# A graph network on one core: ScalarE's and VectorE's pieces laid anew beside TensorE's products

## The chip, the cores and the metric

The kernel runs on one core of one Trainium2 chip, in float32 throughout. The metric is the device time of an execution in microseconds; the time before is the median of three runs. The profile is of one further execution.

## The reference, cut to what matters

Sixteen graphs of 1024 nodes with 512 features each (x), one weighted adjacency matrix adj (1024 x 1024) for all, and two layers with a residual each:

```
# layer 0
h = relu(layernorm(x))
x = x + (adj @ h) @ W0 + bias
# layer 1
u  = relu(layernorm(x))
s1 = (u @ W) @ a1 ; s2 = (u @ W) @ a2
e  = leaky_relu(s1[:, None] + s2[None, :], 0.2) * adj
z  = softmax(e) @ (u @ W) + beta * (u @ W)
x  = x + elu(z)
```

## The kernel before

**Strassen products.** Each big product is done in Winograd's form: seven half-size products p1 to p7 of blocks and of sums of blocks. A left side has the blocks A11, A12, A22, S1 to S4, a right side B11, B21, B22, T1 to T4. In layer 0 the left is h, transposed by the product itself, and the right is the transposed adjacency (adjT); the result y (blocks C11, C12, C21, C22 and their S sums) is the left of a second product with W0 (`Weighted`), whose seven products are added to the residual x one at a time (`to_residual`). Layer 1 has the same two steps with the softmax in place of adjT (tiles pT) and W1 in place of W0.

**Batches in order.** First layer 0 runs for batches 0 to 15, then layer 1 for batches 0 to 15. Each batch of layer 0 has two phases:

- `layer0_a` (batch 0, plain products, 14 half products, "slots" 0 to 13) or `layer0_a2` (batches 1 to 15). In the second, p1, p5, p3 and p4 are split once more into seven small products r1 to r7 (*inner products*), and each is interleaved with a plain one, step by step: p1 with p2, p5 with p6, p3 with p7, p4 with the first product of W0. That gives 4 x 7 = 28 slots, 0 to 27. The loop is at lines 274 to 302. After r1, r5 and r7 ScalarE copies a small result out of PSUM (y_p1t, y_p5t, ... ; r5's copy goes into a buffer named in_p); r6, r7 and r3 end in sums on VectorE. r6 writes into r1's PSUM tile and so waits for r1's copy, and r7 waits for r6's sum. p6 and p7 accumulate in the banks Y that p1 has begun, and so wait until p1's (then p6's) partial result is copied to C11 (C12).
- `layer0_b`: what remains of the seven products with W0, in 14 slots of eight 256-wide matmuls. After each, VectorE adds PSUM to the residual tile xr. Batch 0 takes the products in the order of PRODUCTS (p1, p2, p6, p5, ...), all others in that of A12_LATE (p1, p5, p6, p2, p7, p3, p4).

**What sets the order beside the products.** Every engine takes its instructions in program order (`InOrder`). What ScalarE, VectorE, GpSimd and SP (which issues the DMAs) do beside TensorE is put by hand into *slots*: a plan maps a slot to steps, and `beside(plan)` emits those of slot k after the k-th piece of TensorE's work, slot -1 ahead of the phase. Of one slot, the sums that belong to the product come first, then the plan's. An instruction that waits holds up all behind it on its engine, and a DMA that waits holds up SP. The steps:

- `h_stats` (b, k, c), `h_relu`: layernorm statistics of x chunk k of the next batch (five ScalarE instructions, then small ones on GpSimd), and its normalization with relu on ScalarE. `h_sums`: the sums S1, S2, S4 of h, four VectorE additions for each half. `inner_left`: the sums of one left block for its inner product, four VectorE additions (tiles in_p). `load_x` loads a chunk of x into one of two buffers; `load_res` loads residual rows (xr) into one of four.
- Of `LayerOut` (the result of the batch before): `stats` and `relu` (ScalarE), `logits` (two VectorE products with sums against the vectors v), `sums` (VectorE) and `store` (SP); `keep` stores xr.
- `Softmax` of batch 0 is prepared early: batches 5 to 12 each do one row block g in layer0_b (load of the mask e{g}, M{g}: four ScalarE and four VectorE instructions, K{g}: store). Batch 13 takes the maxima (N, n). Batch 15 reloads the blocks (R{g}, DMA er<-ed) and exponentiates them (E{g}: four ScalarE exponentials, two VectorE transposes). D, d, S, s, T1a to T3b are the rest of the softmax and the sums of its blocks.
- In batch 0 also: `adj_sum` (T1 to T4 of adjT, two VectorE additions each), `w_sums`, `inner_right` (sums of a right block for its inner product, tiles ext), and `logit_weights` (eight VectorE products of W with a1 and a2, then a store vd<-v) with `logit_weights_back` (load of the resulting vectors into v_bc).

`in_fourteen` (line 1067) lays plans made for 28 slots on batch 0's 14 by halving the slot. At lines 1200 and 1201 the plan of slots 0 and 1 of layer0_b is taken over into slots 23 and 26 of layer0_a2.

**Buffers.** Pool b8 has ten slots of one h, adjT or pT block (or of W), b4 twelve smaller ones for y blocks, h sums, small results, masks and e rows; PSUM has eight banks. A tile that finds no free slot waits until one is given back.

## Time and profile before

| what | value |
|---|---|
| time, median of 3 | 2345.65 us (2345.25 to 2348.89) |
| profiled execution | 2345.13 us, span 2343.3 us |
| granted TensorE clock, mean | 0.995 |
| TensorE busy | 2294.7 us (98%) |
| VectorE / ScalarE / GpSimd busy | 1782.8 / 1496.8 / 582.9 us |
| layer 0, batch 0 | 0 to 98.5 us |
| layer 0, batches 1 to 15 | 98.5 to 1170 us |
| layer 1 | 1170 to 2343.3 us |
| DMA | 383.15 MB, mean 164 GB/s |

A line of a timeline has the start and the duration in microseconds, the engine, line, operation, output and inputs by their names in the program with buffer numbers left out, the shapes, how many instructions are merged, and in brackets the idle time ahead of it and what ended it. Line 111 is that of the helper through which every instruction is emitted, so lines are told apart by the tiles' names. In the table of waits, the columns are total, number and longest wait. Matmuls are pipelined and their ends modelled, so the start of one to the start of the next says more than their durations.

### The profile page before, as it was taken

The page shows a single profiled execution, that of the slowest core. Times are in us where ns is not written, and L with a number is a line of the kernel's source. Part 1 is how long each engine was busy: PE and PEld are TensorE (multiplying, and loading weights), DVE is VectorE, ACT ScalarE, POOL GpSimd, SP SyncE. Part 2 cuts the span into 40 slices and gives each one's busy share as a digit, 9 for nine tenths or more (in the row PEclk, how much of TensorE's full clock was granted, in tenths as well). Part 3 has the DMA queues.
Part 4 walks back from the last instruction along what each step waited for, and adds up shares of the span by engine and source line. Part 5 has one row for each costly group of instructions (what it writes and reads, how often), then busy time and mean ns, then how long its engine had stood idle before and what let it go on. Part 6 is the DMA issues. An engine that isn't in the chain of part 4 may idle for free.

```text
span 2343.3 us, 28480 instructions
## 1 busy us (share of the span) xinstructions
PE 2294.7 (98%) x7984; PEld 1511.0 (64%) x7984; DVE 1782.8 (76%) x3932; ACT 1496.8 (64%) x4025; POOL 582.9 (25%) x680
## 2 busy tenths in 40 slices
PE   9899999999999999999899999999999999999998
PEld 5677777777667777677655666556665566655665
DVE  4887777787777787877877787777877778777774
ACT  4565767665767666666357676666766677667743
POOL 1333223333223333232102221122211222102220
PEclk9999999999999999999999999999999999999999
DMA  6254544454543554433754556555565545555541
GB/s 229 64 189 153 171 151 131 153 189 145 171 150 124 168 189 145 163 120 123 245 184 155 166 178 206 173 178 166 189 211 173 186 159 167 179 182 166 175 128 44
DMA packets 207247, 383.15 MB, mean 164 GB/s; under 512 B 80240, under 2 KB 88432, under 8 KB 207088
## 3 DMA queue, kind: packets, MB, share of 16 engines
q1 hardware_dynamic: 206768, 380.81, 49.8%
q8 instruction: 63, 1.03, 0.2%
q14 instruction: 96, 0.79, 0.1%
q10 hardware_dynamic: 320, 0.52, 0.1%
HBM read 251.92 MB, written 133.50 MB: 164 GB/s over the span
## 4 chain that ended last, share of the span: by engine, by line
PE 60%; ACT 14%; DVE 13%; DMA 7%; issue 4%; SPq 2%; POOL 0%; ACTq 0%; DVEq 0%; POOLq 0%
PE z_Y L111 12%; PE y_Y L111 9%; PE pq_Y L111 6%; PE z_X L111 6%; PE po_Y L111 6%; ACT uS L111 5%; PE z_W L111 4%; PE pq_X L111 3%; PE y_X L111 3%; DVE e L111 2%; PE po_X L111 2%; DMA md<-mx 2%; ACT e L111 2%; PE po_W L111 2%; DVE hS L111 2%
## 5 line engine op out<-in xcount | busy, mean ns | idle before, releaser
L111 POOL TENSOR_TENSOR x<-x,r 128x512 f32<-128x512 f32 x120 | 226.0, 1894 | 874.7 <-DVE x L111 432.1
L111 ACT ACTIVATE e<-e,nm 128x256 f32<-128x256 f32 x480 | 237.4, 498 | 162.3 <-DVE nm L111 162.3
L111 DVE CUSTOM_DVE_ANT_0 e<-e,mask 128x256 f32<-128x256 f32 x512 | 233.2, 508 | 66.2 <-DMA mask<-maskd 34.8
L111 POOL TENSOR_TENSOR xr<-xr,bias_bc 128x512 f32<-128x512 f32 x128 | 168.2, 1336 | 269.0 <-DMA xr<-in_x_dram 182.8
L111 PE MATMUL z_Y<-pT,ul_U 128*128 128x512 f32 x512 | 224.9, 592 | 0.0
L111 ACT ACTIVATE e<-s2b,s1b 128x256 f32<-128x256 f32 x512 | 215.1, 506 | 9.0 <-DMA s2b<-s2d 9.0
L111 DVE STREAM_TRANSPOSE pT<-e 128x512 f32<-128x512 f32 x240 | 155.6, 686 | 67.4 <-ACT e L111 67.4
L111 PE MATMUL po_Y<-w_c,y_C 128*128 128x256 f32 x768 | 191.5, 384 | 3.8 <-DVE xr L111 3.8
L111 PE MATMUL pq_Y<-w_c,z_C 128*128 128x256 f32 x768 | 175.4, 380 | 0.6
L111 PEld LDWEIGHTS z_Y<-pT,ul_U 128*128 128x128 f32 x512 | 97.3, 190 | 115.6 <-issue 111.7
L111 DVE CUSTOM_DVE_ANT_0 uS<-xr,v_bc 128x512 f32<-128x512 f32 x240 | 165.7, 691 | 6.2
L111 ACT ACTIVATE r<-z,rs 128x256 f32<-128x256 f32 x192 | 95.7, 499 | 110.9 <-DVE z L111 110.9
L111 PEld LDWEIGHTS pq_Y<-w_c,z_C 128*128 128x128 f32 x768 | 145.1, 190 | 30.4 <-issue 7.7
L111 PEld LDWEIGHTS po_Y<-w_c,y_C 128*128 128x128 f32 x768 | 148.2, 193 | 25.5 <-DVE xr L111 4.2
L111 PE MATMUL y_Y<-adjT_B,h 128*128 128x512 f32 (+1 forms) x332 | 149.7, 554 | 1.6 <-ACT adjT_B L111 1.6
L111 ACT ACTIVATE uS<-xr 128x512 f32<-128x512 f32 x120 | 75.1, 626 | 119.0 <-DVE xr L111 102.7
L111 PE MATMUL y_Y<-adjT_T,hS 128*128 128x512 f32 x256 | 128.9, 599 | 9.8 <-ACT y_C L111 9.8
L111 PE MATMUL y_W<-adjT_B,h 128*128 128x512 f32 x256 | 127.2, 592 | 0.0
L111 ACT ACTIVATE h<-x,nb_h,r_h 128x512 f32<-128x512 f32 (+1 forms) x132 | 98.2, 793 | 44.6 <-POOL nb_h L111 43.4
L111 DVE TENSOR_TENSOR xr<-po_Y,xr 128x512 f32<-128x512 f32 x128 | 87.4, 684 | 41.6 <-PE po_Y L111 38.8
L111 ACT COPY z_C<-z_Y 128x512 f32<-128x512 f32 x96 | 55.5, 578 | 96.9 <-PE z_Y L111 96.9
L111 PE MATMUL po_X<-w_c,y_S 128*128 128x256 f32 x512 | 115.7, 379 | 0.0
(202 smaller groups left out, 4952.8 us busy)
## 6 DMA issues: line engine op xcount, KB each, us to landing
mask<-maskd SPq DMA_DIRECT2D x128, 512.0 KB
x<-in_x_dram SPq DMA_DIRECT2D x64, 512.0 KB
xr<-in_x_dram SPq DMA_DIRECT2D x256, 128.0 KB
x1d<-xr SPq DMA_DIRECT2D x64, 512.0 KB
ul_U<-ud_U SPq DMA_DIRECT2D x64, 512.0 KB
x<-x1d SPq DMA_DIRECT2D x64, 512.0 KB
out_dram<-x SPq DMA_DIRECT2D x252, 128.0 KB
ud_U<-xr SPq DMA_DIRECT2D x60, 512.0 KB
```

The costliest lines, as they stand in the source:

```text
L111: return lambda *args, **kwargs: tc.keep_in_program_order(f(*args, **kwargs))
```

## The change

Only the order of emission and the places of steps change; no arithmetic is added or removed.

- *p2's sum.* In `products_a2` p2's two sums into C11 move from p1's last two steps to the first step of p5.
- *A12_LATE in batch 0.* Its products with W0 are taken in the same order as those of the other batches.
- *Batch 0's slots.* T4 moves to T3's slot 4; `logit_weights` moves from layer0_b's slots 3 and 5 to layer0_a's slot 5, and the load back from batch 1's slot -1 to layer0_b's slot 0. `at_end` replaces `in_fourteen`: the norm of batch 1 goes from slots 4 to 8 into slots 8 to 13.
- *Batches 1 to 15, layer0_a2.* `relu` and `logits` of LayerOut are put in another order, `sums` and `store` of the first half go from slots 10 and 11 to 12 and 13, `inner_left` p5 comes to slot 2, the norm of the next batch goes one to two slots later, and loads move with it.
- *layer0_b.* `h_sums` go from slots 8 and 10 to 7 and 9, `inner_left` p1 from 12 to 11 (p5 is gone from 13), e{g}, M{g}, K{g} from 4, 8, 12 to 2, 5, 10, and `keep` from 12 to 11.
- *Batch 15.* Reloads R5, R6, R7 come earlier.

```diff
             for m in range(7):
                 inn[m]()
                 pla[m if m < 4 else m + 1]()
-                if m == 3:
+                if m == 0 and two == "p5":
+                    reads("p2", 0)
+                    reads("p2", 1)
+                elif m == 3:
                     pla[4]()
                     if one != "p2":
                         reads(one, 0)
                 elif m == 5:
                     reads(two, 0)
-                    if one == "p2":
-                        reads(one, 0)
                 elif m == 6:
-                    for prod in (two, one) if one == "p2" else (one, two):
+                    for prod in (two,) if one == "p2" else (one, two):
                         reads(prod, 1)
...
-            Weighted(f"po{b}", w0_c, partial(to_residual, b)).rest(0, left, beside(plan))
+            Weighted(f"po{b}", w0_c, partial(to_residual, b), A12_LATE).rest(
+                0, left, beside(plan)
+            )
...
-            4: [(adj_sum, "T3")], 5: [(adj_sum, "T4")], 6: [(w_sums, w0_c)],
+            4: [(adj_sum, "T3"), (adj_sum, "T4")],
+            5: [(logit_weights, 0), (logit_weights, 1)], 6: [(w_sums, w0_c)],
...
-        return merged(*({k // 2 if k > 0 else k: v} for k, v in plan.items()))
+        return merged(*({min(4 + k // 2, 13): v} for k, v in plan.items()))
...
-            (3, o.relu, 0, 0), (4, o.stats, 1, 1, 1), (5, o.relu, 1, 0), (6, o.relu, 0, 1),
-            (8, o.relu, 1, 1),
-            (0, inner_left, b, "p3"), (1, inner_left, b, "p4"),
-            (5, o.logits, 0, 0, 0), (7, o.logits, 0, 0, 1),
-            (8, o.logits, 1, 0, 0), (9, o.logits, 1, 0, 1),
-            (10, o.sums, 0, 0), (11, o.sums, 0, 1), (11, o.store, 0),
-            (12, o.logits, 0, 1, 0), (13, o.logits, 0, 1, 1), (13, load_res, b, 0, 0),
-            (14, o.logits, 1, 1, 0), (15, o.logits, 1, 1, 1), (15, load_res, b, 1, 0),
-            (16, o.sums, 1, 0), (17, o.sums, 1, 1), (17, o.store, 1),
-            (19, load_res, b, 0, 1), (21, load_res, b, 1, 1),
+            (3, o.relu, 0, 0), (4, o.stats, 1, 1, 1), (7, o.relu, 0, 1), (8, o.relu, 1, 0),
+            (10, o.relu, 1, 1),
+            (0, inner_left, b, "p3"), (1, inner_left, b, "p4"), (2, inner_left, b, "p5"),
+            (4, o.logits, 0, 0, 0), (5, o.logits, 0, 0, 1), (8, o.logits, 0, 1, 0),
+            (9, o.logits, 0, 1, 1), (10, o.logits, 1, 0, 0), (11, o.logits, 1, 0, 1),
+            (12, o.sums, 0, 0), (13, o.sums, 0, 1), (13, o.store, 0), (14, o.logits, 1, 1, 0),
+            (15, o.logits, 1, 1, 1), (15, load_res, b, 0, 0), (16, o.sums, 1, 0),
+            (16, load_res, b, 1, 0), (17, o.sums, 1, 1), (17, o.store, 1),
+            (20, load_res, b, 0, 1), (21, load_res, b, 1, 1),
...
-            (9, h_stats, b, 0, 0), (10, h_stats, b, 0, 1), (12, h_stats, b, 1, 0),
-            (13, h_stats, b, 1, 1), (14, h_relu, b, 0), (15, load_x, b, 2), (16, h_relu, b, 1),
-            (17, load_x, b, 3),
+            (9, h_stats, b, 0, 0), (11, h_stats, b, 0, 1), (14, h_stats, b, 1, 0),
+            (15, h_stats, b, 1, 1), (16, h_relu, b, 0), (17, load_x, b, 2), (17, h_relu, b, 1),
+            (18, load_x, b, 3),
...
-            (3, h_stats, b, 3, 1), (4, h_relu, b, 2), (6, h_relu, b, 3), (8, h_sums, b, 0),
-            (10, h_sums, b, 1),
+            (3, h_stats, b, 3, 1), (4, h_relu, b, 2), (6, h_relu, b, 3), (7, h_sums, b, 0),
+            (9, h_sums, b, 1), (11, inner_left, b, "p1"),
...
-        return merged(plan, steps((12, inner_left, b, "p1"), (13, inner_left, b, "p5")))
+        return plan
...
-            5 + g: {4: f"e{g}", 8: f"M{g}", 12: f"K{g}" + {3: " X", 7: " x"}.get(g, "")}
+            5 + g: {2: f"e{g}", 5: f"M{g}", 10: f"K{g}" + {3: " X", 7: " x"}.get(g, "")}
...
-        1: "R0", 4: "R1", 7: "B E0 R2", 9: "E1 R3", 12: "E2 R4", 14: "E3", 15: "S b", 17: "R5",
-        21: "R6", 22: "E4",
+        1: "R0", 4: "R1", 7: "B E0 R2", 9: "E1 R3", 12: "E2 R4", 13: "R5", 14: "E3",
+        15: "S b R6", 22: "E4",
...
-        0: "E5", 1: "D R7", 2: "E6", 4: "E7 s", 7: "T1a", 8: "T1b", 10: "d", 11: "T2a",
+        0: "E5 R7", 1: "D", 2: "E6", 4: "E7 s", 7: "T1a", 8: "T1b", 10: "d", 11: "T2a",
...
-                    (11, out_of.stats, 0, 0, 0), (12, out_of.stats, 0, 0, 1),
-                    (13, out_of.stats, 0, 1, 0), (12, out_of.keep, 0, 0),
+                    (11, out_of.stats, 0, 0, 0), (11, out_of.keep, 0, 0),
+                    (12, out_of.stats, 0, 0, 1), (13, out_of.stats, 0, 1, 0),
...
-                    3: [(logit_weights, 0)], 5: [(logit_weights, 1)],
...
-            layer0_a(b, merged(plan_first(), in_fourteen(merged(*plans))))
+            layer0_a(b, merged(plan_first(), at_end(merged(*plans))))
...
-                plans.append({-1: [(logit_weights_back, 0), (logit_weights_back, 1)]})
```

## The prediction

> **What bounds the kernel now.** I read the page first. TensorE is busy 98% of the span at full clock, so only time in which it does not issue can be won.

> ```profile
> span 2343.3 us, 28480 instructions
> PE 2294.7 (98%) x7984; PEld 1511.0 (64%) x7984; DVE 1782.8 (76%) x3932; ACT 1496.8 (64%) x4025; POOL 582.9 (25%) x680
> ```

> Busy time hides slow issue after a wait, so I then took TensorE's timeline and measured start to start: an undisturbed step of two 512-wide or four 256-wide matmuls takes 0.86 us, a 16-matmul block 6.87 (512 wide) or 3.45 (256 wide). What exceeds that is loss. The waits of TensorE say where to look:

> ```profile
> PE y_Y L111 <- ACT y_C L111: 9.8, 9, 1.2
> PE y_p4y L111 <- DVE y_p4t L111: 6.4, 1, 6.4
> PE y_p5y L111 <- ACT y_p5t L111: 5.9, 15, 0.4
> PE po_Y L111 <- DVE xr L111: 4.2, 2, 3.8
> ```

> Three places come out, all in layer 0. *Batch 0*: losses of 1.54 (p4 starts 60.01 instead of 58.47), 0.1, 0.60, 0.11, 3.96 (78.04 to 85.45) and 2.69 (the slow block after it, 6.14 instead of 3.45): **9.0 us**. *Batches 1 to 14*, at the step from p1/p2 to p5/p6. Batch 8, TensorE's timeline:

> ```profile
> 601.64 1.03 PE L111 MATMUL y_p5y<-adjT_T,hS 128*128 128x256 f32 x4
> 603.82 1.13 PE L111 MATMUL y_Y<-adjT_T,hS 128*128 128x512 f32 x2 [1.15 <-ACT y_C L111]
> ...
> 607.37 1.02 PE L111 MATMUL y_Y<-adjT_T,hS 128*128 128x512 f32 x2
> 608.79 1.13 PE L111 MATMUL y_p5y<-ext,in_p 128*128 128x256 f32 x4 [0.40 <-ACT y_p5t L111]
> ```

> That is 2.18 and 1.42 instead of 0.86 twice, and 0.1 behind each: 2.1 us. The y_C wait stands in batches 6 to 13 (and half of it in 14, 1.45 in all); batches 1 to 5 have only the second, 0.7. *Batch 15*: 0.7 there, then 3.2 + 1.6 around 1111.65, 1.1 at 1127.16, and 6.6 + 2.4 around 1144.22: **15.6 us**.

> VectorE's timeline in batch 0 shows the cause of the first:

> ```profile
> 31.81 2.35 DVE L111 TENSOR_TENSOR adjT_B<-adjT_B,adjT_B 128x1024 f32<-128x1024 f32 x2
> 51.80 2.36 DVE L111 TENSOR_TENSOR adjT_T<-adjT_B,adjT_T 128x1024 f32<-128x1024 f32 x2 [17.64 <-PE y_Y L111]
> 54.08 2.61 DVE L111 TENSOR_TENSOR w_c<-w_c 128x512 f32<-128x512 f32 x4
> ```

> T4 is the eleventh tile of the ten-slot pool b8 (B11 to B22, two of h0, w1, T1, T2, then h of batch 1), and waits until p7 has read h0. ScalarE's timeline in batch 15 shows the cause of the last:

> ```profile
> 1140.44 0.51 ACT L111 ACTIVATE er<-er,nm 128x256 f32<-128x256 f32 x1 [5.71 <-DMA er<-ed]
> ```

> [...] after gaps of 3.06, 3.80 and 6.44 us the next 256-wide matmuls come at half pace, for 1.6 to 2.7 us; after 1.15 us they lose 0.1. [...] a product of logit_weights takes 1.63 beside bias additions on GpSimd (79.83) and 0.69 without (86.64).

> **Batch 0.** T4 comes before the next h, so it takes the free slot and runs right behind T3, at 34.16. Behind it on VectorE in the 17.6 us: T4 2.3, logit_weights 8 x 0.72 = 5.8 (GpSimd is idle there; beside it 8 x 1.63, 7.2 more, and p7's first sum would end near 55, still ahead of p4 at 58.47), w_sums 2.5, inner_right p1 2.8: done at 47.6, before p7's first sum is due (48.3). Then 0.6 for that, inner_right p5 2.8, p7's second 0.6, p3's part 2.1, p3's four sums 2.5, p4's part 2.1, four sums 2.5: at about 62.5 all of p3 is read (70.6 to 72.6 now). p4 starts unhindered, and layer0_b has 9.1 us less VectorE work (78.47 to 88.80 less two sums); A12_LATE also asks for C21, the last block, later. All 9.0 us go. The h statistics move from slots 4 to 8 to slots 8 to 13; ScalarE, idle from 48.8 to 63.7 now, takes them (10.1 us with the two relus, 35.12 to 48.78 less the copies between), and the x loads behind them go out near 55 instead of 47.4, with 11 us to their use. SP holds the two v stores from slot 5; only those loads are behind. The load back moves to slot 0 of layer0_b. **-9.0**.

> **Batches 1 to 14.** ScalarE's chain decides p6's start: four statistics, copy, two, copy, one, relu, one, copy, VectorE's y_Y sum, copy to C11. In batch 8 it runs from 586.13 to 603.76 without slack (17.63 us), and the change does not touch its order before that copy. It starts when p3's first sum in layer0_b (slot 10) is done:

> ```profile
> 584.82 0.68 DVE L111 TENSOR_TENSOR xr<-po_Y,xr 128x512 f32<-128x512 f32 x1
> 585.42 0.68 DVE L111 TENSOR_TENSOR xr<-po_X,xr 128x512 f32<-128x512 f32 x1
> 586.02 0.68 DVE L111 TENSOR_TENSOR hS<-h,h 128x512 f32<-128x512 f32 x1
> ```

> Now h_sums stand at slots 8 and 10, the second behind that sum; after the change at 7 and 9, ahead of it. Counted from slot 7's sum at 578.64: 0.6, h_sums 2.53 (to 581.77), two sums 1.2, h_sums 2.53 (585.50), sum done 586.2. The mask work (1.38), now at slot 5, no longer adds. So in batches 6 to 13 the chain starts where it did (+0.07) and p6's wait stays, 1.4. In batches 1 to 5, without mask work, the same count from 297.27 gives 304.8 against 303.34: 1.47 later, with about 0.1 of slack (C11 ends 321.00, p6 starts 321.13): a new wait of 1.4. What does go is p5's wait: relu(1,0) and relu(0,1), 1.5 each, no longer stand ahead of p5's first copy, which falls to about 606.2 against 608.38, and p2's sums no longer sit between VectorE's two y_Y sums (0.65 waits of VectorE each). So every batch loses 1.5: batches 6 to 13 8 x -0.6 = **-4.8**, 1 to 5 5 x +0.8 = **+4.0**. Batch 14 has the top maxima (0.8) between h_sums and that sum: 2.3, **+0.9**. Holding p2's two banks into p5 leaves four of eight PSUM banks for the three that p5 takes; if one is p1's own, p5's first matmul waits 0.8 for its copy (to 602.42), inside p6's wait: nothing. inner_left p5 at slot 2 costs VectorE 1.46 where it has 4.6 idle (before 602.45): nothing.

> DMA: on SP the load of x chunk 2 moves behind the second store (issue 622.22 now, then about 631.8). With 5.5 us to landing, as for the er reload of batch 15 (1134.96 to 1140.44), it comes at 637 where ScalarE wants it at 633.5. Behind it wait p4's last copy (due 637.5) and the statistics; relu 2 comes 1.4 later, and h_sums need it only at slot 7, 5 us on. The first store comes 4.7 later (its sums at slots 12, 13), xr with it, still 8 us before its use at 635.6. **0**; uncovered, each us would cost a us a batch.

> **Batch 15.** p6's wait 1.5. In p5, E0's and E1's transposes still stand ahead of the sum that p5's r7 waits for (E0's exps end later, as relu(0,1) comes first): 3.0 plus 1.6. p3: 0.9. E5's reload now goes out at slot 13, behind the first store, near 1122 instead of 1134.96, so E5 runs behind E4 and VectorE's sum for p4 is done at 1139.8 instead of 1144.2; TensorE reaches that point at about 1138, so 1.9 stays, plus up to 1.6 of slow clock, taken as 1.0. In all 10.0 instead of 15.6: **-5.6**.

> Sum: -9.0 - 4.8 + 4.0 + 0.9 - 5.6 = -14.5. The profiled execution took 2345.13 (span 2343.3 and 1.8 around it), 0.5 under the median; I take the sum from the median: 2345.65 - 14.5 = **2331 us**. Layer 1's order is not touched.

> **Rivals.** *ScalarE's chain is early enough everywhere* (18%): if the first statistics don't wait for the second h_sums, as where they are interleaved differently than I count, the steps of batches 1 to 14 lose nothing: 8 x 2.1 + 5 x 0.7 + 1.45 = 21.7 won, with batch 0 and about 7 in batch 15: -38, 2308. For it speaks that both waits hang on ScalarE, against it the in-order count above. *One end doesn't come* (12%): T4 still finds no free slot, or E5's reload waits for a b4 buffer: 5.6 to 9 less, 2337 to 2340. *Slower* (12%): the second h_sums, now ahead of p3's sum, wait for ScalarE's relu 3, itself behind x chunk 3 and GpSimd's bias additions; then VectorE's whole queue, and ScalarE's chain with it, start late in each of 14 batches. It decides from 14.5/14 = 1.04 us a batch; at 2 us, +13.5: 2359. Against it: I count 4 us of margin (relu 3 at about 650, needed at 654). *Nothing measurable* (3%): 2345. The rest, 55%, is the forecast, 2324 to 2339 on its own (1.5 us a part, 0.3 us in each of 14 batches).

> A change of 0.2%, 4.7 us, is about what can be told here. Faster: 55 + 18 + 11 = 84%; slower 11%; same 5%. The range from 2312 to 2347 leaves out some 8% below and 11% above.

> **What would show it.** T4 at 34 with no 17.6 us gap on VectorE, and no po_Y wait for xr; the wait of y_Y for y_C in 14 or 15 batches, each near 1.2, and none of p5 for its copy; E5's exps right behind E4's. Wrong would be: the y_C wait gone from batches 1 to 5; gaps over 1.5 on p6 (relu 3 late); new waits of po_Y for xr.

## The result, and the profile after

The kernel after the change takes 2373.08 us (median of four runs, 2369.25 to 2378.0), the kernel before, beside it, 2346.73 (2345.25 to 2348.89): a ratio of 1.0113, 95% interval 1.0092 to 1.0134. It is 26 us slower, where 2331 was predicted with a range from 2312 to 2347. The profiled execution took 2372.76 us, with a span of 2371.0.

The page of the kernel after, its span and first table:

```profile
span 2371.0 us, 28526 instructions
PE 2301.4 (97%) x7984; PEld 1510.0 (64%) x7984; DVE 1802.4 (76%) x3932; ACT 1499.6 (63%) x4025; POOL 572.2 (24%) x680
```

The work is the same and so is the granted clock, 0.995 in both; TensorE has more pauses. Its waits after the change (total, number, longest):

```profile
PE y_p1y L111 <- ACT y_p1t L111: 27.7, 15, 2.3
PE y_Y L111 <- ACT y_C L111: 13.3, 10, 1.3
PE po_Y L111 <- DVE xr L111: 3.7, 4, 2.5
...
PE y_p4y L111 <- DVE y_p4t L111: 2.2, 1, 2.2
```

The first line is new: p1's r6 now waits in all 15 batches for ScalarE's copy of r1, which the kernel before did not have to wait for. The wait of p5 for its copy (15 times) is gone, as predicted.

Measured start to start as in the prediction, in the one profiled execution of each kernel, TensorE's losses add up to 62.0 us before and 89.4 after, in these places:

| place | before | after | predicted change | measured change |
|---|---|---|---|---|
| batch 0, from 23 us | 9.2 | 0.3 | -9.0 | -8.9 |
| batches 1 to 15, the first 25 us (p1/p2, p5/p6) | 22.6 | 56.4 | about +1 | **+33.8** |
| batch 15, after these | 15.0 | 12.7 | -6.4 | -2.3 |
| rest of layer 0 | 7.2 | 9.5 | 0 | +2.3 |
| layer 1 | 8.0 | 10.5 | 0 | +2.5 |

The sum is +27.4, against 27.7 in the spans. One row decides. VectorE's timeline in batch 0 after the change, which shows the row that came as predicted (T4, right behind T3, and `logit_weights` behind it):

```profile
34.37 2.35 DVE L111 TENSOR_TENSOR adjT_T<-adjT_B,adjT_T 128x1024 f32<-128x1024 f32 x2
36.64 0.68 DVE L111 CUSTOM_DVE_ANT_0 junk<-w_t,v_bc 128x512 f32<-128x512 f32 x1
```

TensorE's timeline in batch 8, the same place as shown before the change:

```profile
605.50 1.13 PE L111 MATMUL y_p1y<-ext,in_p 128*128 128x256 f32 x4 [2.30 <-ACT y_p1t L111]
...
613.35 1.03 PE L111 MATMUL y_p5y<-adjT_T,hS 128*128 128x256 f32 x4
615.71 1.12 PE L111 MATMUL y_Y<-adjT_T,hS 128*128 128x512 f32 x2 [1.33 <-ACT y_C L111]
```

2.46 us are lost ahead of r6 and 1.50 ahead of p6, both behind ScalarE: 4.17 with what follows, where it was 2.1. (p6 waits in 10 batches; in the other five, slow matmuls behind r6's pause, at a granted clock of 0.50, take as much, 1.7 to 1.8 us.) ScalarE, in the same batch:

```profile
586.59 1.52 ACT L111 ACTIVATE h<-x,nb_h,r_h 128x512 f32<-128x512 f32 x2 [0.81 <-POOL nb_h L111]
598.02 0.63 ACT L111 ACTIVATE uS<-xr 128x512 f32<-128x512 f32 x1 [9.92 <-DVE xr L111]
```

Its chain of statistics starts at 598.02, when TensorE has begun p1 (597.87), after 9.92 us of idle time for VectorE's xr. And VectorE, ahead of that:

```profile
587.81 0.69 DVE L111 TENSOR_TENSOR xr<-po_W,xr 128x512 f32<-128x512 f32 x1 [1.39 <-POOL xr L111]
589.04 0.69 DVE L111 TENSOR_TENSOR xr<-po_W,xr 128x512 f32<-128x512 f32 x1 [0.53 <-POOL xr L111]
589.65 1.14 DVE L111 TENSOR_TENSOR hS<-h,h 128x512 f32<-128x512 f32 x1
590.82 1.64 DVE L111 TENSOR_TENSOR hS<-hS,h 128x512 f32<-128x512 f32 x1
592.38 0.68 DVE L111 TENSOR_TENSOR h<-h 128x512 f32<-128x512 f32 x1
...
593.59 1.27 DVE L111 TENSOR_TENSOR xr<-po_Y,xr 128x512 f32<-128x512 f32 x2
...
597.30 1.28 DVE L111 TENSOR_TENSOR xr<-po_X,xr 128x512 f32<-128x512 f32 x2
```

The order is the one the prediction counted with: p2's sums, first h_sums, two sums, second h_sums, and only then the sum of p3 (xr<-po_X) that ScalarE waits for. The sizes are not. p2's sums wait for GpSimd, and the first two additions of h_sums take 1.14 and 1.64 instead of 0.68. GpSimd's timeline there:

```profile
586.36 0.19 POOL L111 TENSOR_TENSOR nb_h<-mv_h,r_h 128x2 f32<-128x2 f32 x1
586.51 5.40 POOL L111 TENSOR_TENSOR xr<-xr,bias_bc 128x512 f32<-128x512 f32 x4
```

The four bias additions of the first column half run from 586.51 to 591.91: p2's sums wait for the first two, and the first h_sums lie beside the last two. In batch 15, ScalarE's E5 (1160.82, right behind E4) and E7:

```profile
1160.82 0.51 ACT L111 ACTIVATE er<-er,nm 128x256 f32<-128x256 f32 x1
1180.36 0.51 ACT L111 ACTIVATE er<-er,nm 128x256 f32<-128x256 f32 x1 [10.69 <-DMA er<-ed]
```

E5's gap of 5.71 us is gone; E7, whose reload did not hold anything up before, now waits 10.69 us for it.

### The profile page after: what moved, and what is told of

Read it like the earlier page. It is cut to its first block, busy times and chain, and to the rows that moved or that the text cites. A ratio compares the mean times of both kernels' runs of the same rounds, so it can differ in the third digit from the quotient of the medians.

```text
span 2371.0 us, 28526 instructions
## 1 busy us (share of the span) xinstructions
PE 2301.4 (97%) x7984; PEld 1510.0 (64%) x7984; DVE 1802.4 (76%) x3932; ACT 1499.6 (63%) x4025; POOL 572.2 (24%) x680
## 3 DMA queue, kind: packets, MB, share of 16 engines
q8 instruction: 63, 1.03, 0.2%
## 4 chain that ended last, share of the span: by engine, by line
PE 50%; DVE 17%; DMA 12%; ACT 11%; POOL 4%; issue 3%; SPq 3%; DVEq 0%; ACTq 0%; POOLq 0%
PE z_Y L111 11%; PE y_Y L111 9%; PE pq_Y L111 5%; PE z_X L111 5%; PE y_X L111 4%; PE z_W L111 3%; ACT e L111 3%; DVE hS L111 3%; DMA md<-mx 3%; SPq L111 3%; DVE in_p L111 3%; DVE e L111 3%; DVE xr L111 3%; ACT uS L111 2%; POOL xr L111 2%
## 5 line engine op out<-in xcount | busy, mean ns | idle before, releaser
L111 POOL TENSOR_TENSOR x<-x,r 128x512 f32<-128x512 f32 x120 | 226.1, 1895 | 880.1 <-DVE x L111 433.0
L111 ACT ACTIVATE e<-e,nm 128x256 f32<-128x256 f32 x480 | 237.4, 498 | 165.6 <-DVE nm L111 165.6
L111 DVE CUSTOM_DVE_ANT_0 e<-e,mask 128x256 f32<-128x256 f32 x512 | 237.7, 517 | 71.3 <-DMA mask<-maskd 43.9
L111 POOL TENSOR_TENSOR xr<-xr,bias_bc 128x512 f32<-128x512 f32 x128 | 169.5, 1345 | 266.7 <-DMA xr<-in_x_dram 181.1
L111 PE MATMUL z_Y<-pT,ul_U 128*128 128x512 f32 x512 | 224.9, 592 | 0.0
L111 ACT ACTIVATE e<-s2b,s1b 128x256 f32<-128x256 f32 x512 | 215.2, 507 | 11.7 <-DVE pT_T L111 11.7
L111 DVE STREAM_TRANSPOSE pT<-e 128x512 f32<-128x512 f32 x240 | 155.7, 687 | 68.3 <-ACT e L111 68.2
L111 DVE CUSTOM_DVE_ANT_0 uS<-xr,v_bc 128x512 f32<-128x512 f32 x240 | 165.5, 690 | 41.1 <-ACT xr L111 33.9
L111 PE MATMUL po_Y<-w_c,y_C 128*128 128x256 f32 x768 | 190.0, 381 | 3.2 <-DVE xr L111 3.2
L111 PE MATMUL pq_Y<-w_c,z_C 128*128 128x256 f32 x768 | 176.7, 381 | 3.1 <-DVE z L111 1.5
L111 ACT ACTIVATE uS<-xr 128x512 f32<-128x512 f32 x120 | 75.1, 626 | 153.0 <-DVE xr L111 151.6
L111 PEld LDWEIGHTS z_Y<-pT,ul_U 128*128 128x128 f32 x512 | 97.3, 190 | 115.6 <-issue 112.6
L111 PEld LDWEIGHTS pq_Y<-w_c,z_C 128*128 128x128 f32 x768 | 144.5, 190 | 35.0 <-issue 7.7
L111 ACT ACTIVATE r<-z,rs 128x256 f32<-128x256 f32 x192 | 95.8, 499 | 111.3 <-DVE z L111 111.3
L111 PEld LDWEIGHTS po_Y<-w_c,y_C 128*128 128x128 f32 x768 | 145.8, 191 | 25.6 <-DVE xr L111 5.4
L111 PE MATMUL y_Y<-adjT_B,h 128*128 128x512 f32 (+1 forms) x332 | 149.9, 555 | 1.8 <-ACT adjT_B L111 1.8
L111 PE MATMUL y_Y<-adjT_T,hS 128*128 128x512 f32 x256 | 128.2, 596 | 13.3 <-ACT y_C L111 13.3
L111 PE MATMUL y_W<-adjT_B,h 128*128 128x512 f32 x256 | 133.0, 617 | 0.0
L111 ACT ACTIVATE h<-x,nb_h,r_h 128x512 f32<-128x512 f32 (+1 forms) x132 | 98.3, 794 | 40.0 <-POOL nb_h L111 40.0
L111 PE MATMUL po_X<-w_c,y_S 128*128 128x256 f32 x512 | 116.5, 381 | 0.0
L111 PE MATMUL pq_X<-w_c,z_S 128*128 128x256 f32 x512 | 115.8, 379 | 0.0
L111 PE MATMUL z_X<-pT_T,ul_S 128*128 128x512 f32 x256 | 112.5, 592 | 0.0
```

What stands on the lines that cost most here:

```text
L111: return lambda *args, **kwargs: tc.keep_in_program_order(f(*args, **kwargs))
```

## The experiments

The table holds what the experiments turn on, averaged over the eight layer0_b of batches 5 to 12 (which feed the steps of batches 6 to 13) and counted in us from the first matmul of p2's block (po_W): the end of p2's second sum, how long the first h_sums take, and the start of ScalarE's chain. "Loss" is TensorE's loss in the first 25 us of batches 1 to 15, all together. These four columns come from one profiled execution of each kernel. Ratios are to the kernel before on the same chip, with the 95% interval.

| kernel | p2's sums | first h_sums | chain | loss | time | ratio |
|---|---|---|---|---|---|---|
| before | 4.42 | 2.61 | 11.22 | 22.6 | 2346.73 | 1 |
| after | 5.57 | 3.98 | 13.83 | 56.4 | 2373.08 | 1.0113 (1.0092-1.0134) |
| e1, x chunk 2 early | 5.81 | 4.01 | 14.10 | 60.9 | 2379.82 | 1.0136 (1.0121-1.0151) |
| e2, h_sums at 8, 10 | 5.90 | 3.53 | 11.21 | 16.7 | 2333.18 | 0.9939 (0.9925-0.9954) |
| e3, two bias additions first | 4.97 | 4.74 | 14.00 | 59.0 | 2373.98 | 1.0113 (1.0098-1.0128) |
| e5, before, h_sums at 7, 9 | 4.42 | 3.72 | 13.80 | 61.5 | 2381.16 | 1.0161 (1.0133-1.0189) |
| e6, h_sums at 7, 10 | 5.80 | 3.84 | 11.39 | 19.4 | 2332.00 | 0.9949 (0.9934-0.9964) |
| e7, h_sums at 10, 11 | 5.87 | 2.61 | 9.57 | 2.6 | 2313.88 | 0.9873 (0.9851-0.9895) |
| e9, two bias slots later | 6.10 | 3.80 | 14.18 | 58.3 | 2378.56 | 1.0137 (1.0121-1.0152) |
| e13, four additions left out | 4.35 | 2.61 | 11.24 | 22.7 | 2337.55 | 0.9957 (0.9941-0.9974) |
| e14, two additions left out | 5.97 | 2.61 | 12.86 | 39.9 | 2356.59 | 1.0043 (1.0029-1.0056) |

**e1: the load of x chunk 2 ahead of the second store.** From the traces my first theory was the late load: it makes ScalarE's statistics late, GpSimd's r_h behind these, and the bias additions behind r_h.

```diff
-            (15, h_stats, b, 1, 1), (16, h_relu, b, 0), (17, load_x, b, 2), (17, h_relu, b, 1),
+            (15, h_stats, b, 1, 1), (16, h_relu, b, 0), (16, load_x, b, 2), (17, h_relu, b, 1),
```

> The kernel after, with one DMA moved: the load of x chunk 2 goes out one slot earlier, ahead of the second store on SP. Theory A (the late load sets off the chain: late statistics on ScalarE, late r_h on GpSimd, late bias additions behind it, VectorE's sums of p2 wait for these, and h_sums with ScalarE's chain come late): VectorE's waits of xr for GpSimd fall from 29.2 to about 16 us, ScalarE's first statistics come about 2.5 us earlier a batch, the losses of TensorE at p1's r6 and p6 from 4.1 to about 1.5 us a batch, and the time falls by 30 to 38 us, to 2335 to 2343. Theory B (h_sums ahead of p3's first sum cost that much by themselves, whenever x arrives): under 7 us won, 2366 to 2373. Mixed: half a batch's loss stays, about 2355.

Measured: 2379.82, slower still. The load came earlier, as the waits show, first after, then e1:

```profile
ACT h L111 <- DMA x<-in_x_dram: 41.5, 15, 4.5
DVE xr L111 <- POOL xr L111: 29.2, 25, 3.5
DVE xr L111 <- DMA xr<-in_x_dram: 4.8, 7, 1.5
```

```profile
ACT h L111 <- DMA x<-in_x_dram: 8.2, 13, 1.3
DVE xr L111 <- POOL xr L111: 36.4, 28, 4.0
DVE xr L111 <- DMA xr<-in_x_dram: 13.7, 20, 1.3
```

ScalarE hardly waits for x any more, but now the residual rows, which SP issues next, come late instead, and VectorE's sums and GpSimd's additions wait for these. So this run alone doesn't decide theory A: what one load won, others lost. e5 and e7, below, say more: e5 loses as much without any wait of ScalarE for x, and e7 loses almost nothing in that place with 37.8 us of such waits. So a late load is not needed for such a loss, and alone it makes none.

**e2: h_sums back at 8 and 10.**

```diff
-            (3, h_stats, b, 3, 1), (4, h_relu, b, 2), (6, h_relu, b, 3), (7, h_sums, b, 0),
-            (9, h_sums, b, 1), (11, inner_left, b, "p1"),
+            (3, h_stats, b, 3, 1), (4, h_relu, b, 2), (6, h_relu, b, 3), (8, h_sums, b, 0),
+            (10, h_sums, b, 1), (12, inner_left, b, "p1"),
```

> The kernel after, with h_sums back at slots 8 and 10 (and inner_left of p1 at 12), so that the second h_sums stand behind p3's first sum again; the load of x chunk 2 stays late. Theory A (the late load): p2's sums still come 1.5 us late, but the second h_sums, 2.6 to 4 us, no longer lie between them and ScalarE's chain; the chain starts about 1.5 us later than before the change, losses of about 2 to 2.5 us a batch, 2345 to 2350. Theory B (the order of h_sums alone): all of the 2.9 us a batch comes back, losses of about 1 us a batch, 2325 to 2332. If neither matters (the order in the step with the inner products is the cause): within 7 us of 2373.

Measured: 2333.18, 40 us below after and faster than before. p2's sums are as late as in after and the first h_sums still stretched (3.53), yet ScalarE's chain starts at 11.21. So what carries the delay on is the second h_sums' place ahead of p3's first sum.

**e3: two bias additions ahead of r_h of chunk 3.**

```diff
-                    (0, 0, 1), (0, 1, 1), (1, 0, 1), (1, 1, 1), (0, 0, 0), (0, 1, 0), (1, 0, 0),
+                    (0, 0, 1), (0, 1, 1), (0, 0, 0), (0, 1, 0), (1, 0, 1), (1, 1, 1), (1, 0, 0),
```

> The kernel after, with GpSimd's bias additions for (0,0) and (0,1), first half, at slots 2 and 3 and those for (1,0) and (1,1), second half, at 4 and 5: p2's sums then have their bias ahead of GpSimd's r_h of chunk 3. The load stays late, h_sums stay ahead of p3's sum. Theory A, if GpSimd's queue is the link: p2's sums follow TensorE again, the chain starts about 1.5 us earlier, losses of 2.6 instead of 4.1 us a batch, about 2352. If ScalarE's late relu 2 and 3 are the link instead (h_sums wait for relu 3): no more than 5 us won.

Measured: 2373.98, nothing won, although VectorE's waits of xr for GpSimd fall from 29.2 to 2.9 us. In batch 8 VectorE's h_sums show what took their place:

```profile
592.96 1.64 DVE L111 TENSOR_TENSOR hS<-hS,h 128x512 f32<-128x512 f32 x1
594.52 1.75 DVE L111 TENSOR_TENSOR h<-h 128x512 f32<-128x512 f32 x1
596.20 1.75 DVE L111 TENSOR_TENSOR hS<-h,hS 128x512 f32<-128x512 f32 x1
```

They now start at 592.12, 0.8 us earlier than in after when counted from p2's block, beside the whole run of GpSimd's additions, and take 5.8 us. A wait was traded for a slowdown. Neither alternative I had written down covers that.

**e4: batch 0 alone**, on the kernel before.

```diff
-            4: [(adj_sum, "T3")], 5: [(adj_sum, "T4")], 6: [(w_sums, w0_c)],
+            4: [(adj_sum, "T3"), (adj_sum, "T4")],
+            5: [(logit_weights, 0), (logit_weights, 1)], 6: [(w_sums, w0_c)],
...
-            Weighted(f"po{b}", w0_c, partial(to_residual, b)).rest(0, left, beside(plan))
+            Weighted(f"po{b}", w0_c, partial(to_residual, b), A12_LATE).rest(
```

> The kernel before with the edits of batch 0 alone (T4 behind T3, logit_weights at slot 5 and back at slot 0 of layer0_b, A12_LATE in batch 0, the rest of its plan at slots 4 to 13). By the prediction's step for batch 0: no 17.6 us gap ahead of T4, TensorE's 9.0 us of loss there gone, all else as before: 2337 (-9). A rival: half of it comes back as losses in batch 1, 2341.

Measured: 2337.89, ratio 0.9955 (0.9939 to 0.9972), 7 to 14 us won. TensorE's loss in batch 0 falls from 9.2 to 0.2 us, and batches 1 to 15 lose 23.0, as before.

**e5: h_sums at 7 and 9 alone**, on the kernel before.

```diff
-            (3, h_stats, b, 3, 1), (4, h_relu, b, 2), (6, h_relu, b, 3), (8, h_sums, b, 0),
-            (10, h_sums, b, 1),
+            (3, h_stats, b, 3, 1), (4, h_relu, b, 2), (6, h_relu, b, 3), (7, h_sums, b, 0),
+            (9, h_sums, b, 1),
```

> The kernel before with one edit of the change alone: h_sums at slots 7 and 9 instead of 8 and 10. By the prediction's count (h_sums at 2.53 us each, nothing beside them): ScalarE's chain 0.07 later in batches 6 to 13 and 1.4 later in 1 to 5, +8 to +10, about 2356. If the first h_sums, now beside GpSimd's four bias additions, are stretched by 0.9 to 1.5 us: 1.0 to 1.5 later in batches 6 to 13 and 2.4 to 3 in 1 to 5, +20 to +30, 2367 to 2377. If h_sums matter only with the rest of the change: within 5 of 2347.

Measured: 2381.16, +35 us, above even the second alternative. This one edit, without anything else of the change, makes as large a loss: 61.5 us in batches 1 to 15 instead of 22.6. Here p2's sums are on time; the first h_sums take 3.72, and the mask work, which in this kernel stands behind them at slot 8, adds its 1.4.

**e6: only the second h_sums back** (7 and 10).

```diff
-            (9, h_sums, b, 1), (11, inner_left, b, "p1"),
+            (10, h_sums, b, 1), (12, inner_left, b, "p1"),
```

> The kernel after with only the second h_sums moved back behind p3's first sum (slots 7 and 10); the first stay at slot 7, beside the bias additions. If the order of the second h_sums to that sum is the cost: the chain starts about 11.6 us after p2's block starts, 1.0 us later than with both moved back and 2.5 earlier than after, 2340 to 2348. If the first h_sums' stretch beside GpSimd is the larger part: 2355 to 2365.

Measured: 2332.00, not told apart from e2. The stretch of the first h_sums is still there (3.84), and the chain starts at 11.39: the place of the second h_sums is worth 2.4 us a batch.

**e7: both h_sums behind p3's sums** (10 and 11).

```diff
-            (3, h_stats, b, 3, 1), (4, h_relu, b, 2), (6, h_relu, b, 3), (7, h_sums, b, 0),
-            (9, h_sums, b, 1), (11, inner_left, b, "p1"),
+            (3, h_stats, b, 3, 1), (4, h_relu, b, 2), (6, h_relu, b, 3), (10, h_sums, b, 0),
+            (11, h_sums, b, 1), (12, inner_left, b, "p1"),
```

> The kernel after with both h_sums behind p3's sums (slots 10 and 11, inner_left of p1 at 12). If ScalarE's chain is set by whatever VectorE does ahead of p3's first sum, this sum runs as soon as TensorE has its bank (1.4 us earlier than with slots 8 and 10), nothing is beside GpSimd's additions, and p6's wait for y_C goes: 2318 to 2324. Against it: the first left sums of p1 come about 1 to 2 us later, and r5 and r6 of p1 may wait for these: 2325 to 2340.

Measured: 2313.88, better than the first alternative. VectorE's timeline there, and ScalarE's first statistics behind it:

```profile
567.65 0.69 DVE L111 TENSOR_TENSOR xr<-po_X,xr 128x512 f32<-128x512 f32 x1 [1.03 <-PE po_X L111]
568.26 0.68 DVE L111 TENSOR_TENSOR hS<-h,h 128x512 f32<-128x512 f32 x1
```

```profile
568.37 0.63 ACT L111 ACTIVATE uS<-xr 128x512 f32<-128x512 f32 x1 [6.65 <-DVE xr L111]
```

p3's first sum now waits for TensorE alone (1.03), the chain starts at 9.57 in every batch, and neither r6 nor p6 nor p5 waits in batches 1 to 14. p1's left sums come in time. (p2's sums are late here too, at 5.87; why is not shown. ScalarE's chain does not feel it.)

**e8: e2, with R7 ahead of the residual loads in batch 15.**

```diff
-        15: "S b R6", 22: "E4",
+        15: "S b R6", 19: "R7", 22: "E4",
...
-        0: "E5 R7", 1: "D", 2: "E6", 4: "E7 s", 7: "T1a", 8: "T1b", 10: "d", 11: "T2a",
+        0: "E5", 1: "D", 2: "E6", 4: "E7 s", 7: "T1a", 8: "T1b", 10: "d", 11: "T2a",
```

> The kernel after with h_sums at 8 and 10 and, in batch 15, the reload of the last exponent tile (R7) at slot 19, ahead of the residual loads, instead of behind these and the loads for layer 1. If VectorE's transposes of E7 behind the late reload are what holds TensorE in layer0_b of batch 15: the 2.5 us gap there (and slow matmuls after it) goes, 3 us less than with h_sums back alone, 2329 to 2331. If the residual loads, now later, take its place: the same as that, 2333.

Measured: 2332.41 (0.9954, 0.9935 to 0.9972), the same as e2. TensorE's gap behind E7 (2.5 us) goes, but the gap ahead of p4's r7 grows from 2.1 to 2.6 us, and one of 1.5 comes in layer0_b, where VectorE's sum has waited 2.42 us for its residual rows (1.07 in e2). So the residual loads, now behind R7, take a part of what was won, as the second alternative had it; what makes r7's gap grow is not shown.

**e9: the last two bias additions at slots 10 and 11.**

```diff
-                (k, add_bias, b, *t) for k, t in enumerate((
+                (k, add_bias, b, *t) for k, t in zip((0, 1, 2, 3, 4, 5, 10, 11), (
```

> The kernel after with GpSimd's last two bias additions, (1,0) and (1,1) of the first half, at slots 10 and 11 instead of 6 and 7: h_sums at 7 and 9 stay where they are, only the work beside the first of them goes. [...] these take 2.6 to 2.9 us, ScalarE's chain starts 1.2 to 1.4 us earlier in each batch, 2352 to 2356. If the stretch doesn't matter: within 5 of 2373.

Measured: 2378.56, nothing won, and no verdict on the stretch of the first h_sums beside GpSimd's additions (3.80 here, 3.98 in after, 2.61 in before): the additions did not move in time. GpSimd's timeline in e9, in the next batch, where h_sums begin at 666.70:

```profile
663.55 5.41 POOL L111 TENSOR_TENSOR xr<-xr,bias_bc 128x512 f32<-128x512 f32 x4
```

In this program a slot orders a step on its engine and holds it back for nothing else. GpSimd has nothing to do between these slots, so the additions run as soon as their residual rows are there.

**e13 and e14: additions left out.** e13 leaves out all four bias additions of the first column half, e14 the last two of these.

```diff
-                    (0, 0, 1), (0, 1, 1), (1, 0, 1), (1, 1, 1), (0, 0, 0), (0, 1, 0), (1, 0, 0),
-                    (1, 1, 0),
+                    (0, 0, 1), (0, 1, 1), (1, 0, 1), (1, 1, 1),
```

> The kernel after without GpSimd's four bias additions of the first half of the output columns (left out in every batch; h_sums at 7 and 9, all else as after). It takes the work away that stands ahead of p2's sums and beside the first h_sums. If these additions are what my count left out: p2's sums end 4.4 us after p2's block starts, the first h_sums take 2.6 us, the chain starts at the 11.3 of my count instead of 13.8, losses of 1.3 to 1.5 us a batch, 2335 to 2342. If something else stretches the first h_sums or holds p2's sums: the chain stays above 12.5 and the time above 2355.

> The kernel after without the last two of these four additions, (1,0) and (1,1); the two that p2's sums wait for stay. Only the work beside the first h_sums goes. If GpSimd beside VectorE stretches them: 2.6 us instead of 4.0, p2's sums still 1.1 us late, the chain at 12.4, losses of 2.6 us a batch, 2350 to 2358. If the stretch has another cause: within 5 of 2373.

Measured: 2337.55 and 2356.59, both within the first range expected. With none of the four, h_sums take 2.61 at the same slots and the chain starts at 11.24, where the prediction's count had put it; with the first two kept, h_sums take 2.61 and p2's sums stay late. So after's 2.6 us (13.83 against 11.24) are the 1.4 of the stretch (3.98 to 2.61), which the additions beside h_sums make, and the 1.2 of p2's sums (5.57 to 4.35), which wait for the other two. In e14 the chain gains 1.0 and not 1.4, since p2's sums are 0.4 later still; why is not shown.

**e10 to e12: what the rest of the change is worth** once h_sums are at 10 and 11. e10 is the kernel before with these slots and the edits of batch 0, nothing else.

```diff
-            (3, h_stats, b, 3, 1), (4, h_relu, b, 2), (6, h_relu, b, 3), (8, h_sums, b, 0),
-            (10, h_sums, b, 1),
+            (3, h_stats, b, 3, 1), (4, h_relu, b, 2), (6, h_relu, b, 3), (10, h_sums, b, 0),
+            (11, h_sums, b, 1),
```

> The kernel before with the edits of batch 0 and h_sums at slots 10 and 11, and nothing else of the change (ScalarE's and VectorE's order beside the inner products, p2's sums and batch 15 as before). If the two waits of each batch are independent, as the prediction had it: p6's wait for y_C goes (8 of 1.4 us and one of 0.75), p5's wait for its copy stays (15 of 0.7), batch 0 gives 9: 2325. If p5's wait goes too with an earlier chain: 2314.

Measured: 2322.42, ratio 0.9894 (0.9879 to 0.9909). p6's wait goes, and p5's stays, at half its size, since the chain is earlier:

```profile
PE y_p5y L111 <- ACT y_p5t L111: 2.6, 15, 0.2
```

e11 is e7 with p2's sums back in the first step:

```diff
-                if m == 0 and two == "p5":
-                    reads("p2", 0)
-                    reads("p2", 1)
-                elif m == 3:
+                if m == 3:
...
                     reads(two, 0)
+                    if one == "p2":
+                        reads(one, 0)
```

> The kernel after with h_sums at 10 and 11, and p2's two sums back in the step of p1 and p2, between the two sums of y_Y. If p2's move buys VectorE's 0.65 to 1.3 us on the way to y_C: p6 waits 0.3 to 0.9 us again in 15 batches, 2319 to 2327. If ScalarE's chain now has that much room: 2314, as with p2's sums moved.

Measured: 2316.44, ratio 0.9869 (0.9852 to 0.9885), not told apart from e7; no wait of p6 or p5 comes back. e12 is e7 with the slots of the layer output and of the next h's first half as before the change:

```diff
-            (3, o.relu, 0, 0), (4, o.stats, 1, 1, 1), (7, o.relu, 0, 1), (8, o.relu, 1, 0),
-            (10, o.relu, 1, 1),
+            (3, o.relu, 0, 0), (4, o.stats, 1, 1, 1), (5, o.relu, 1, 0), (6, o.relu, 0, 1),
+            (8, o.relu, 1, 1),
...
-            (9, h_stats, b, 0, 0), (11, h_stats, b, 0, 1), (14, h_stats, b, 1, 0),
+            (9, h_stats, b, 0, 0), (10, h_stats, b, 0, 1), (12, h_stats, b, 1, 0),
```

> The kernel after with h_sums at 10 and 11, and the slots of the layer output (statistics, relus, logits, sums, stores, residual loads) and of the next h's first half as before the change; p2's sums and inner_left of p5 as after. If the two relus ahead of p5's first copy are what p5 waits for: 15 waits of 0.4 to 0.7 us come back, 2320 to 2325. If the earlier chain alone takes that wait away: 2314; the stores and loads, which go out earlier, could also win 1 or 2 us.

Measured: 2307.14, ratio 0.9834 (0.9818 to 0.9850), the fastest of all kernels here (span 2304.1 us, TensorE busy 99% of it).

Here p5 waits in no batch up to 14 either, with the two relus ahead of its first copy again. In batch 8, counted from p1's start, that copy starts at 18.01 in e10 (both as before), at 16.58 in e11 (the relus in their new order), at 16.64 in e12 (p2's sums moved) and at 15.24 in e7 (both). TensorE asks for it at about 18.1. So each of the two edits brings it 1.4 us forward, and either is enough once the chain is early. The new order of the layer output brings nothing beside p2's move. e12's lead over e7, 6.7 us, stands in TensorE's losses in batch 15 (8.1 against 9.9 us) and in layer 1 (6.6 against 11.0). But in the kernels profiled here layer 1, whose order none of them changes, loses anything from 5.1 to 16.7 us. So most of that lead is not shown to come from the edit.

## Why the prediction was wrong

**Batch 0, -9.0: right.** T4 runs at 34.37 behind T3, the 17.64 us gap is gone, 8.9 us are won, and e4 shows them alone.

**Batches 1 to 14: the step that failed.** The prediction named the decisive point, h_sums "ahead of p3's first sum", and priced it: "0.6, h_sums 2.53 (to 581.77), two sums 1.2, h_sums 2.53 (585.50), sum done 586.2", so that the chain starts "where it did (+0.07)". It started 2.6 us later in batches 6 to 13, and 3.5 later in 1 to 5, where 1.47 was counted. The mis-sized terms are two. The first "h_sums 2.53" measured 3.98, because they came to lie beside GpSimd's bias additions; "slot 7's sum at 578.64" came 1.15 us later, because p2's sums wait for such additions. e13 takes both away and the count holds (11.24; 11.29 was counted). The price of such a stretch was in the prediction, 1.63 against 0.69 us, and was used in batch 0, where it was harmless, but not for h_sums, where it decides. The traces show which of VectorE's instructions it concerned: h_sums, with both inputs in SBUF, go from 0.68 to 1.64 and 1.75 (after, e3) and back to 0.68 without the additions (e14), while p2's sums, with one input in PSUM, take 0.69 in the middle of them (587.81 and 589.04 in after, within GpSimd's 586.51 to 591.91). So which steps may lie beside GpSimd's additions could have been read off the trace of before. The products of `logit_weights`, with both inputs in SBUF, took the 1.63, and p2's second sum, ahead of batch 8, took 0.69:

```profile
578.64 0.69 DVE L111 TENSOR_TENSOR xr<-po_W,xr 128x512 f32<-128x512 f32 x1 [0.65 <-PE po_W L111]
```

It lies within GpSimd's additions. When these run could be read too:

```profile
576.00 4.96 POOL L111 TENSOR_TENSOR xr<-xr,bias_bc 128x512 f32<-128x512 f32 x4
```

They end at 580.96. The h_sums of before start at 580.91, as they end; the prediction's count put the first h_sums at 579.24 to 581.77, in part beside them.

**"A new wait of 1.4" in batches 1 to 5, 1.5 in all others: too small.** TensorE's loss there measured 2.3 to 4.3 a batch, since what the chain starts late TensorE loses nearly in full. The first part of it appears at p1's r6, for the copy of r1, which the prediction did not look at: it took p6 as the only place where the chain is felt.

**p5's wait goes: right**, and so are both causes it gave, the two relus and p2's sums. With an early chain either alone would do (e11, e12).

**"DMA: ... 0": wrong as a statement on the load, which alone costs nothing.** ScalarE waits 41.5 us for x after the change, where the waits of before have no such line. But e5 loses as much without that wait, and e13 with it (48.5 us) loses no more than before. What late loads can have added in after is the 1.15 us of p2's sums.

**Batch 15, -5.6 (p6's +0.8 included): right in mechanism.** E5 runs behind E4, and p4's r7 waits 2.19 instead of 6.44. With the late chain taken out (e7), batch 15 loses 9.9 where the prediction had 10.0 (by chance: 1.5 of these were for p6's wait, which e7 has not). What it missed is R7: E7 waits 9.97 us in e7 and 10.69 in after, and TensorE, in layer0_b behind VectorE's transposes of E7, loses 2.85 and 4.46. Other terms of after were off both ways: p5's loss was 2.55 against 4.6, p3's 2.0 against 0.9.

**The rivals.** *Slower* had the right place and the right law (VectorE's queue, then ScalarE's chain, late in each batch, deciding from about 1 us), with the wrong agent: after batch 0 h_sums never waited for relu 3 (done at 588.11, h_sums start at 589.65 in batch 8, so 1.5 us are left of the 4 counted). *ScalarE's chain early enough everywhere*, at 2308, is about the time of e12, which came there by h_sums going behind p3's sums and not ahead.

**Open.** Layer 1 loses 2.5 us more and the rest of layer 0 2.3 more than before; with the spread of layer 1 told above, its part says nothing of the change. And GpSimd's four additions start 2.1 us after p2's block in after, 0.8 in before; which loads set that, and with it the 1.15 us of p2's sums, was not separated: e1 moved one and another took its place.

## What to carry to other kernels

On a queue taken in order, ask of each step what on another engine waits for the one behind it: h_sums could go 4 us later at no cost (e7), p3's sum had nothing to spare, and which of them comes first was worth 59 us (after to e7). When a step is moved, look again at what runs on GpSimd at its new time, and price it beside that work and not by its old duration (the first h_sums 3.98 us instead of 2.61); here the sums out of PSUM, 0.69 us in both places, are the ones that could stay there. A slot later in the plan did not mean later in time on an engine that was idle (e9: the additions ran from 663.55 to 668.96, still beside h_sums), and on SP's queue one load's advance was the next ones' delay (e1: waits for x fell from 41.5 to 8.2 us, VectorE's for residual rows rose from 4.8 to 13.7).

## What was not expected of the hardware

Where h_sums on VectorE and the bias additions on GpSimd lay beside each other, both took longer, and h_sums by more. In e3's batch 8 VectorE's four additions take 5.8 us instead of 2.6, 3.2 more, and GpSimd's four beside them 6.30 instead of 4.96, 1.3 more:

```profile
591.10 6.30 POOL L111 TENSOR_TENSOR xr<-xr,bias_bc 128x512 f32<-128x512 f32 x4
```

One after another the eight would take 2.61 + 4.96 = 7.57 us; from 591.10 to the end of VectorE's last at 597.95 are 6.85. So they overlap by some 0.7 us of the time that the profile counts, and VectorE bears most of the loss. Why is not shown.

The length of a pause did not tell whether TensorE's clock fell behind it. The prediction had read half pace behind gaps of 3.06 us and more, and 0.1 us lost behind 1.15. After the change the same pause of 2.30 us ahead of r6 stands in batches 4 and 8. Four stretches of the kernel after, for each batch one with the pause and one right behind it (window, length, busy time and instructions of each engine, granted clock, DMA share, GB/s):

```profile
311.46:314.87 3.41, 1.13 (x4) 0.28 (x2) 3.34 (x10) 3.25 (x12) 1.18 (x4) 1.00 0.60 239
314.90:317.50 2.60, 2.60 (x5) 1.84 (x6) 0.14 (x1) 2.47 (x8) 1.07 (x3) 0.50 0.00 0
601.59:605.00 3.41, 1.61 (x6) 0.70 (x4) 3.32 (x10) 3.25 (x10) 1.29 (x3) 1.00 0.76 299
605.50:608.00 2.50, 2.50 (x8) 1.63 (x9) 0.14 (x1) 2.37 (x8) 1.07 (x3) 1.00 0.02 7
```

In batch 4 the clock is halved (0.50), in batch 8 it is whole (1.00). It is halved too in batches 7, 10, 12 and 15, the shortest of these pauses being 1.88 us. In these five batches 1.7 to 1.8 us go to slow matmuls, and p6, reached later, does not wait: the sum stays at 3.9 to 4.3 us.
